# Four GNN layers over 16 batches: one layer's rows emitted beside the next batch's one-hot builds, with one scratch pool

## The chip, the cores and the metric

The kernel runs on one core of a Trainium2 chip. The metric is device time in microseconds (us), from the first to the last instruction of one execution; less is better. The engines are PE (TensorE, matmuls; PEld is its weight load), DVE (VectorE), ACT (ScalarE), POOL (GpSimd) and SP, which issues most transfers.

## The reference, cut to what matters

There are 16 batches of 1024 nodes with 128 features and a dense-stored, sparse 1024 x 1024 adjacency. Four layers run one after the other, each with a normalization ahead of it and a residual around it. Batches do not depend on each other, which is all that the change uses.

```python
x   : (16, 1024, 128) float32
adj : (16, 1024, 1024) float32, about 1.6% set, symmetric pattern, diagonal set

for layer in (L0, L1, L2, L3):
    h = maximum(layernorm(x), 0)
    x = x + layer(h, adj)

# L0: relu(concat(h, adj^T h / degree) W0^T + b0)
# L1: leaky_relu((adj / degree) h W1^T + b1)
# L2: twice: a score per edge (sigmoid of a small MLP of both ends), messages, update, layernorm
# L3: Wh = h W;  e = leaky_relu((Wh a1 + (Wh a2)^T) * (adj + I))
#     attention = softmax over the row of where(adj + I > 0, e, -1e12);  elu(attention Wh)
```

## The kernel before

The kernel treats edges, not all node pairs, in layer 2. For this it makes one-hot matrices from the adjacency, block by block, while it transposes the adjacency; I call row block `s` of this "build s". Eight builds give the transposed adjacency, the one-hots of 36 block pairs, and layer 0's neighbour sums (`acc`). Layer 2 is then two passes over eight groups of block pairs. Layer 3 walks over eight row blocks; I call each "row t".

Buffers come from pools by tag. All [128, 8, 128] float32 working tiles share tag `h` (6 buffers before), and all large PSUM tiles share tag `ps` with two buffers.

```python
def scratch(self, name):
    return self.work.tile([P, T, P], F32, tag="h", name=name, bufs=self.n_scratch)   # 6

def ps(self, name):                                                 # bufs=2
    return self.psum.tile([P, T, P], F32, tag="ps", name=name)

def layer0_own(self, xt, name):
    _, hT = self.pre_ln(xt, f"0_{name}")        # center, power on GpSimd, norm, 8 transposes, copy
    z = self.scratch(f"z0_{name}")
    nc.scalar.activation(z, self.by_node(hT, wT[:, 1], f"z0_{name}"), AF.Copy)
    own = self.scratch(f"own_{name}")
    nc.vector.tensor_add(own, self.by_node(hT, wT[:, 0], f"own_{name}"), over_t(b0_bc))
    return z, own

def layer3(self, xt, row, name):
    ...                                          # norm, wh, wh1, wh2: "the head"
    for t in range(T):                           # one row of layer 3
        at = row(t)                              # adjacency row, loaded again
        own = at[:, t * P : (t + 1) * P]
        nc.vector.tensor_add(own, own, ident)
        e = flat(self.scratch(f"e_{name}_{t}"))
        nc.vector.scalar_tensor_tensor(e, wh2, wh1[:, t : t + 1], at, op0=OP.add, op1=OP.mult)
        nc.vector.tensor_scalar(at, at, 0.0, L3_NEG, op0=OP.is_le, op1=OP.mult)
        nc.vector.scalar_tensor_tensor(e, e, L3_ALPHA, e, op0=OP.mult, op1=OP.max)
        nc.vector.tensor_add(e, e, at)
        nc.vector.tensor_reduce(nmax, e, axis=AX.X, op=OP.max, negate=True)
        nc.scalar.activation(e, e, AF.Exp, bias=nmax, accum_out=rsum[:, 0, t : t + 1])
        ps = self.ps(f"attT_ps_{name}_{t}")
        for k in range(T):
            nc.tensor.transpose(ps[:, k], e[:, k * P : (k + 1) * P], ident)
        attT = self.scratch(f"attT_{name}_{t}")
        nc.scalar.activation(attT, ps, AF.Copy)
        hp = self.one(f"hp_{name}_{t}")[:, :D]
        for k in range(T):
            nc.tensor.matmul(hp, attT[:, k], wh[:, k], start=(k == 0), stop=(k == T - 1))
        nc.vector.reciprocal(rsum[:, 1, t : t + 1], rsum[:, 0, t : t + 1])
        nc.vector.tensor_scalar(o[:, t], hp, rsum[:, 1, t : t + 1], None, op0=OP.mult)
    ...                                          # elu and residual: "the tail"

def batch(self, b):
    xt = ...                                     # load x[b]
    z, own = self.layer0_own(xt, f"{b}")
    for s in range(T):
        at = self.load_row(b, s, "at")
        nc.vector.tensor_reduce(deg[:, s : s + 1], at, axis=AX.X, op=OP.add)
        ps = self.ps(f"aT_{b}_{s}")
        for k in range(T):
            nc.tensor.transpose(ps[:, k], at[:, k * P : (k + 1) * P], ident)
        nc.scalar.activation(adjT[:, :, s * P : (s + 1) * P], ps, AF.Copy)
        for t in range(T):
            nc.tensor.matmul(acc[:, t * P : (t + 1) * P], at[:, t * P : (t + 1) * P], z[:, s], ...)
        self.build(s, at, adjT, f"{b}_{s}")      # begins with has = at OR adjT on VectorE
    self.layer0_end(xt, acc..., own, rdeg, f"{b}")
    self.layer1(xt, adjT, rdeg, f"{b}")          # begins with its own pre_ln
    self.layer2(xt, self.edge, f"{b}")           # edge: for grp in self.groups(): ...
    self.layer3(xt, lambda t: self.load_row(b, t, "a3"), f"{b}")
    ...                                          # store
```

## Time and profile before

| | before |
|---|---|
| median of 3 runs | 8855.1 us (8854.83 to 8858.05) |
| mean granted TensorE clock | 0.820 |
| one batch, end of layer 2 to end of layer 2 | 549.4 us |
| of it, layer 2 up to its last update | 267.2 us |
| of it, everything else | 282.2 us |
| loads of activation tables | 16 for Exp, 16 for Sigmoid |

Four kinds of views are used beside the page of a profile. The waits name, for an engine and a line, what ended its idle time; the numbers are us in total, how often, and the longest. The busy time by stretch gives the first and last moment of a stretch, its length, then busy us and count of instructions for PE, PEld, DVE, ACT and POOL, then the granted clock (1.00 is full), the share of DMA time and GB/s. The timeline lists start, length, engine and line of each piece of work, with the idle time before it in brackets and what ended that. The chain of work follows the work that ended last back from releaser to releaser, and lists start, length, engine, tile and line of each piece.

The busy time by stretch of the first two builds in the middle of the run, from the first VectorE operation of one build (`has`) to that of the next:

```profile
5004.40:5010.70 6.30, 6.30 (x65) 6.07 (x64) 3.47 (x10) 2.86 (x5) 0.00 (x0) 1.00 0.22 83
5010.70:5017.70 7.00, 6.36 (x65) 5.66 (x64) 4.64 (x13) 3.46 (x7) 0.00 (x0) 1.00 0.22 78
```

Build 0 and build 1 take 6.3 and 7.0 us. The later builds, with more blocks each, take 7.8, 10.7, 14.4, 15.9, 15.4 and 17.5 us.

### The profile page before, as it was taken

The page shows a single profiled execution, that of the slowest core. Times are in us where ns is not written, and L with a number is a line of the kernel's source. Part 1 is how long each engine was busy: PE and PEld are TensorE (multiplying, and loading weights), DVE is VectorE, ACT ScalarE, POOL GpSimd, SP SyncE. Part 2 cuts the span into 40 slices and gives each one's busy share as a digit, 9 for nine tenths or more (in the row PEclk, how much of TensorE's full clock was granted, in tenths as well). Part 3 has the DMA queues.
Part 4 walks back from the last instruction along what each step waited for, and adds up shares of the span by engine and source line. Part 5 has one row for each costly group of instructions (what it writes and reads, how often), then busy time and mean ns, then how long its engine had stood idle before and what let it go on. Part 6 is the DMA issues. An engine that isn't in the chain of part 4 may idle for free.

```text
span 8857.3 us, 112984 instructions
## 1 busy us (share of the span) xinstructions
PE 6284.3 (71%) x48784; PEld 4682.8 (53%) x48784; DVE 4389.8 (50%) x7991; ACT 2760.4 (31%) x4099; POOL 158.9 (2%) x105
## 2 busy tenths in 40 slices
PE   6857668576685767857678586776867768677686
PEld 5645456454554555545455454555545555455454
DVE  4454454545545455454554545445455454544544
ACT  3233242232423224232242322423224232242322
POOL 0000000000000000000000000000000000000000
PEclk8968779687896878969789697896978969789697
DMA  1010000100001000010000100001000010000100
GB/s 40 1 38 6 15 29 1 39 5 16 28 1 41 3 17 27 1 43 1 20 25 1 43 1 20 25 1 43 1 20 25 1 43 1 22 22 1 41 1 15
DMA packets 75915, 160.16 MB, mean 18 GB/s; under 512 B 6929, under 2 KB 42641, under 8 KB 75409
## 3 DMA queue, kind: packets, MB, share of 16 engines
q1 hardware_dynamic: 70144, 151.01, 5.4%
q8 instruction: 385, 6.31, 0.3%
q10 hardware_dynamic: 5264, 1.84, 0.1%
q14 instruction: 122, 0.99, 0.0%
HBM read 144.45 MB, written 8.39 MB: 17 GB/s over the span
## 4 chain that ended last, share of the span: by engine, by line
PE 64%; DVE 19%; ACT 13%; issue 2%; POOL 1%; DMA 1%; ACTq 0%; DVEq 0%; POOLq 0%; SPq 0%
PE pre L616 8%; PE sc L635 7%; PE pre L620 7%; PE p L686 7%; PE hp L323 5%; PE msg L713 5%; PE attT_ps L318 3%; PE h L262 3%; PE ga L211 3%; PE acc L746 2%; ACT hid L625 2%; ACT e L315 2%; DVE nmax L314 2%; DVE e L312 2%; ACT attT L320 1%
## 5 line engine op out<-in xcount | busy, mean ns | idle before, releaser
L625 ACT ACTIVATE hid<-pre,be_sb 128x640 f32<-128x640 f32 (+1 forms) x1152 | 880.8, 765 | 1958.2 <-PE pre L620 1939.7
L647 DVE TENSOR_SCALAR s_off<-sc,be_s 128x320 f32<-128x320 f32 x224 | 123.4, 551 | 1325.1 <-PE sc L635 1325.1
L318 PE MATMUL attT_ps<-ident,e 128*128 128x128 f32 x1024 | 252.1, 428 | 596.0 <-ACT e L315 596.0
L668 DVE TENSOR_TENSOR val<-onT,u 128x384 f32<-128x384 fp8e4 (+1 forms) x1152 | 653.4, 583 | 8.8
L635 PE MATMUL sc<-hid,slide_s 128*32 128x320 f32 (+1 forms) x4096 | 627.1, 461 | 30.3 <-ACT hid L625 30.2
L686 PE MATMUL p<-val,omT 128*128 128x128 f16 x7424 | 622.1, 218 | 10.3 <-DVE val L668 10.3
L323 PE MATMUL hp<-wh,attT 128*128 128x128 f32 x2048 | 477.1, 427 | 150.5 <-ACT attT L320 150.5
L620 PE MATMUL pre<-om,part_b 128*128 128x320 fp8e4 (+1 forms) x2304 | 540.4, 314 | 47.4 <-DVE part_b L548 28.2
L616 PE MATMUL pre<-on,part_a 128*128 128x320 fp8e4 (+1 forms) x2304 | 538.9, 315 | 32.0 <-DVE part_a L548 2.0
L686 PEld LDWEIGHTS <-omT 128*128 128x128 fp8e4 x7424 | 506.7, 96 | 85.0 <-issue 16.6
L323 PEld LDWEIGHTS hp<-wh,attT 128*128 128x128 f32 x2048 | 442.4, 328 | 201.7 <-ACT attT L320 201.7
L318 PEld LDWEIGHTS attT_ps<-ident,e 128*128 128x128 f32 x1024 | 200.9, 224 | 643.5 <-ACT e L315 643.5
L713 PE MATMUL msg<-upd,xf 128*128 128x128 f32 (+3 forms) x2944 | 539.5, 322 | 1.8 <-DVE upd L709 1.1
L668 DVE TENSOR_TENSOR val<-omT,u 128x384 f32<-128x384 fp8e4 x896 | 495.7, 553 | 0.0
L177 PE MATMUL tp<-ident,h 128*128 128x128 f32 x384 | 88.4, 408 | 549.2 <-DVE h L184 549.2
L713 PEld LDWEIGHTS msg<-upd,xf 128*128 128x128 f32 x2944 | 407.0, 191 | 121.0 <-DVE upd L709 65.3
L686 PE MATMUL p<-val,onT 128*128 128x128 f16 x5376 | 450.9, 218 | 0.0
L616 PE MATMUL pre<-on,part_b 128*128 128x320 fp8e4 x1792 | 423.4, 299 | 0.0
L531 DVE TENSOR_TENSOR omT<-pq,odd 128x384 fp8e4<-128x384 f32 (+1 forms) x576 | 329.4, 584 | 183.0 <-PE pq L528 174.5
L178 ACT ACTIVATE hT<-tp 128x1024 f32<-128x1024 f32 x64 | 65.5, 1023 | 1133.0 <-PE tp L177 1133.0
L315 ACT ACTIVATE e<-e,nmax 128x1024 f32<-128x1024 f32 x128 | 146.8, 1147 | 816.2 <-DVE nmax L314 816.2
L620 PE MATMUL pre<-om,part_a 128*128 128x320 fp8e4 x1792 | 394.8, 299 | 0.0
(202 smaller groups left out, 11164.3 us busy)
## 6 DMA issues: line engine op xcount, KB each, us to landing
at<-in_adj_dram SPq DMA_DIRECT2D x128, 512.0 KB, 3.5
a<-in_adj_dram SPq DMA_DIRECT2D x128, 512.0 KB, 3.5
x<-in_x_dram SPq DMA_DIRECT2D x16, 512.0 KB, 4.0
out_dram<-x SPq DMA_DIRECT2D x16, 512.0 KB, 3.2
wu_sb<-in_L_gnn_Wu_dram ACTq DMA_DIRECT2D x2, 256.0 KB, 5.9
we_sb<-in_L_gnn_We_dram ACTq DMA_DIRECT2D x2, 128.0 KB, 5.5
wu_sb<-in_L_gnn_Wu_dram ACTq DMA_DIRECT2D x2, 128.0 KB, 5.4
w_sb<-in_L_gnn_W_dram ACTq DMA_DIRECT2D x2, 64.0 KB, 3.2
```

The costliest lines, as they stand in the source:

```text
L211: nc.tensor.matmul(ps[:, t], mat[:, k, t * P : (t + 1) * P], z[:, k], start=(k == 0), stop=(k == T - 1),)
L315: nc.scalar.activation(e, e, AF.Exp, bias=nmax, accum_out=rsum[:, 0, t : t + 1])
L318: nc.tensor.transpose(ps[:, k], e[:, k * P : (k + 1) * P], ident)
L323: nc.tensor.matmul(hp, attT[:, k], wh[:, k], start=(k == 0), stop=(k == T - 1))
L531: nc.vector.tensor_tensor(omT, pq[:, :ck], self.odd[:, :ck, None].to_broadcast([P, ck, P]), op=OP.is_equal, saturate=False,)
L616: nc.tensor.matmul(pre[:, d, :c], ra[0][:, k, ra[1]], on[:, :c], start=(k == 0), stop=False)
L620: nc.tensor.matmul(pre[:, d, :c], rb[0][:, k, rb[1]], om, start=False, stop=(k == 1))
L625: nc.scalar.activation(hid, pre[:, :nd, :c], AF.Relu, bias=be1_sb[:, self.l : self.l + 1])
L635: nc.tensor.matmul(self.sc[g * G : (g + 1) * G, : self.c], self.path.slide[:, self.l, G - 1 - r : 2 * G - 1 - r], self.hid[self.done + g], ...
L668: nc.vector.tensor_tensor(val[:, :ck], right, u[:, :, i % J, i // J : i // J + 1].to_broadcast([P, ck, P]), op=OP.mult,)
L686: nc.tensor.matmul(self.ps[:, d * len(self.grp) + i], left[:, k], halves[:, k, :, h], start=(k == 0 and h == 0), stop=(k == self.ck - 1 an ...
L713: nc.tensor.matmul(self.msg[:, lo * P : hi * P], self.xf[:, mb], upd, start=False, stop=True, skip_group_check=True,)
```

## The change

The intent is to run the two chains of short dependent steps, layer 3's rows of batch b and the builds of batch b + 1, beside each other: after each build, one row is emitted. So that build 0 can begin at once, the start of batch b + 1 (its load, norm and layer 0's own part) moves into layer 2 of batch b, before group 3 of the second pass. Layer 3's tail moves behind layer 1. Because the lifetimes of buffers now cross, the scratch tiles, the split features of layer 2, the edge values and the adjacency rows of layer 3 all draw on one pool of 11.

```diff
-    z, own = self.layer0_own(xt, f"{b}")        # in batch(b)
+def start(self, b):
+    xt = ...                                    # load x[b]
+    return xt, *self.layer0_own(xt, f"{b}")
+
+def att_row(self, b, t, att):
+    at = flat(self.scratch(f"a3_{b}_{t}"))      # was: load_row, from the builds' three buffers
+    nc.sync.dma_start(at, adj[b, t * P : (t + 1) * P, :])
+    self.layer3_row(att, t, at, f"{b}")

# edge(), the group loop of layer 2
-    for grp in self.groups():
+    for k, grp in enumerate(self.groups()):
+        if k == 3 and l == L - 1:
+            self.during()                       # start(b + 1)

# run(), for every batch
+    att = self.layer3_head(last, f"{b - 1}") if b else None
     for s in range(T):
         ...                                     # transposes, acc
         self.build(s, at, adjT, f"{b}_{s}")
+        if b:
+            self.att_row(b - 1, s, att)
     self.layer0_end(...)
     self.layer1(xt, adjT, rdeg, f"{b}")
+    if b:
+        self.end(b - 1, last, att)              # layer 3's tail, store
     self.layer2(xt, self.edge, f"{b}")
-    self.layer3(xt, lambda t: self.load_row(b, t, "a3"), f"{b}")

# buffers
-    super().__init__(stack, 6, None)
+    super().__init__(stack, 11)                 # parts, values, wh, o and rows now come from these
-    hT = self.work.tile([P, T, P], F32, tag="hT", name=f"hT_{name}", bufs=1)
+    hT = self.work.tile([P, T, P], F32, tag="hT", name=f"hT_{name}")     # two
... (cut: layer3 split into head, row and tail; values taken in pairs)
```

## The prediction

> **What bounds the kernel now.** I read the page first (engine shares, slices), then the waits, then the busy time by stretch for one batch in the middle, then the chain of work in order of time across that batch.
>
> The page's engine shares and two of its slice rows (tenths busy, granted TensorE clock in tenths):
>
> ```profile
> PE 6284.3 (71%) x48784; PEld 4682.8 (53%) x48784; DVE 4389.8 (50%) x7991; ACT 2760.4 (31%) x4099; POOL 158.9 (2%) x105
> ...
> PE   6857668576685767857678586776867768677686
> ...
> PEclk8968779687896878969789697896978969789697
> ```
>
> No engine is full; the pattern repeats 16 times, once per batch, and the clock dips each time. One period is 549.4 us (end of layer 2 in one batch to the same point in the next). Its stages, cut where the chain changes layer: last feature update of layer 2, head of layer 3, the eight rows of layer 3, layer 0 of the next batch, the one-hot builds, the rest of layer 1, then layer 2 to the last update:
>
> ```profile
> core 0: us, PE busy (x) PEld busy (x) DVE busy (x) ACT busy (x) POOL busy (x), PEclk, DMA share, GB/s
> 4841.00:4867.50 26.50, 11.10 (x57) 7.29 (x55) 12.58 (x12) 2.23 (x2) 1.64 (x1) 0.80 0.00 0
> 4867.50:4892.70 25.20, 10.83 (x48) 7.84 (x48) 10.16 (x13) 3.10 (x4) 1.64 (x1) 0.67 0.00 1
> 4892.70:4984.10 91.40, 45.50 (x192) 40.15 (x192) 52.33 (x65) 19.37 (x25) 0.00 (x0) 0.57 0.15 46
> 4984.10:5002.50 18.40, 7.43 (x42) 7.06 (x43) 7.83 (x9) 3.10 (x3) 1.64 (x1) 0.63 0.20 58
> 5002.50:5099.40 96.90, 70.16 (x642) 57.09 (x640) 64.34 (x154) 62.90 (x125) 1.64 (x1) 0.79 0.13 44
> 5099.40:5123.20 23.80, 16.61 (x144) 16.23 (x144) 4.87 (x4) 2.03 (x3) 0.00 (x0) 1.00 0.00 1
> 5123.20:5390.40 267.20, 229.27 (x1936) 155.57 (x1936) 122.17 (x245) 79.78 (x97) 3.27 (x2) 0.94 0.00 1
> ```
>
> The reader is to see two regimes. The last row (layer 2) is TensorE-bound: 229 of 267 us busy at clock 0.94. In the other 282.2 us nothing is bound by an engine; these are chains of latencies, and rows and builds (91.4 + 96.9 us) are two such chains run one after the other. One row of layer 3 in the chain of work:
>
> ```profile
> 4906.98 1.14 DVE e L312
> 4908.15 1.23 DVE nmax L314
> 4909.40 1.25 ACT e L315 x2
> 4910.69 1.99 PE attT_ps L318 x8
> 4912.76 1.03 ACT attT L320
> 4913.84 3.79 PE hp L323 x16
> 4918.01 1.14 DVE e L312
> ```
>
> Here 11.0 us pass per row, each engine waiting for the previous one. VectorE has the eviction of the row's product ahead of the next row's add, so it too waits for the matmuls.
>
> **What the Trainium skill says.** "Perfetto Trace Analysis", Optimization Strategy, advises interleaving regimes whose most-contended engine differs: this is the change's intent, and the table agrees that there is room (52 + 64 us of VectorE in 188 us). The same page, Tensor Engine Instruction, says ACT and DVE are strict FIFO and PE reorders only weight loads; the row above agrees (VectorE idles 2.7 us before that eviction in every row while the add behind it has its operands). "TensorE: Matmul & The Clock Gate", Part 1, says idle time halves the clock; the trace agrees: eight fp32 128x128 transposes take 1.98 us in the rows (clock 0.57) and 0.88 us in the builds. "ScalarE: Activation LUTs", Table sets, says a switch of set costs a load of about 1283 ns and that abs, relu and copy are in every set: the trace has loads of 1283 ns, 16 for Exp and 16 for Sigmoid, so one of each per batch, and none between the last Exp and the builds' Abs and Copy. Mixing rows with builds should therefore add no table loads.
>
> **The change part by part**, per batch boundary; there are 15 of them, since the last batch's layer 3 still stands alone and the first batch's builds too.
>
> *Removed: layer 0's own part in the open.* Its 18.4 us (mean, norm, transposes, two products) move into the second edge pass of layer 2, before group 3: −18.4.
>
> *Removed: rows and builds in series*: −91.4 −96.9 = −188.3. *Added: both together.* VectorE has most to do. Rows: 52.3 us less three degree sums of the next batch (3 x 1.22) plus three diagonal adds that ran elsewhere (3 x 0.29) = 49.6. Builds: 64.3 plus 3.6 for those sums, less the end of layer 0 (3 x 1.22), the pre-norm of layer 1 (7.5) and the three diagonal adds (0.9) = 55.9. Together 105.5. ScalarE has 19.4 + 62.9 = 82, and TensorE 45.5 at half clock (some 22 warm) + 70 = 92. So no engine forbids 106 us. But orders are kept: rows and builds draw on the same two PSUM buffers, and the trace suggests that buffers of one tag are given in the code's order. Layer 1's normalized input is ready at 5063, yet its transposes wait for the last build's matmuls:
>
> ```profile
> 5061.90 1.13 DVE h L184
> ...
> 5095.82 0.51 PE pq L524 x4
> 5096.33 0.43 PE pq L528 x4
> 5096.76 1.71 PE tp L177 x8
> ```
>
> So build s+1 starts after row s is transposed, and a row has 5.9 us of VectorE plus 1.3 of Exp ahead of that, which must squeeze into the gaps of build s (6 to 17 us long). I choose 80% busy for VectorE (the builds alone reach 66%, with one chain): 105.5 / 0.8 = 132. Net −56.
>
> *Moved: end of layer 0 and pre-norm of layer 1.* They ran hidden inside builds 6 and 7. They take scratch buffers, which now come after row 7's in the code's order, so I expect them in the open: 3 + 6 VectorE operations of about 1.22 and the power on GpSimd 1.8 = +13.
>
> *Added to layer 2: the start of the next batch.* If its scratch and PSUM buffers come in the code's order, group 3's first gather follows the two products of the start. Group 2's scores and eight multiplies (0.55+0.5+0.4+3.8) come first, then about 7 us of mean, square, power and norm, 1 of transposes, 1 of copy, 2 + 1.8 of products: some 18 us in which TensorE has only about 2 us of messages to do. +16. If the norm slips into VectorE's 6 us gaps in group 2, this is only +6.
>
> *Added at the end: layer 3's tail*, four operations after layer 1's, mixed with layer 2's norm: +3. The rest (11 scratch buffers for values, parts and updates, two buffers for the transposed input) I count as zero: layer 2's multiplies waited only 8.8 us in all, so buffers did not bind, and two parts + four pairs + two updates are 8 of 11.
>
> Sum per boundary: −18.4 −188.3 +132 +13 +16 +3 = −42.7 us. Times 15: −640. 8855 − 640 = 8215 us.
>
> **Rivals.**
> (a) *Nearly perfect overlap.* VectorE 92% busy (115 us) and only +6 in layer 2: −70 per boundary, 7805 us. For it: TensorE warms up, so a row's matmul part shrinks from 5.8 to some 2.8 us. Against it: strict order in each queue and two PSUM buffers for four kinds of users.
> (b) *The rows are slotted between the builds rather than beside them.* Each step of build then row takes build plus some 8 us: 88 + 64 = 152, −23 per boundary, 8510 us. For it: shared PSUM order. Against it: a row's first five operations need no PSUM and VectorE idles a third of each build.
> (c) *Scratch becomes the bound.* In the joint stretch z, own, wh, wh2 and o hold five of 11; in layer 2 the held z and own leave nine. If multiplies wait for a pair, TensorE in layer 2 starves, and 5% of layer 2's 267 us is 13 us. With (b) that gives about 8700, no gain to speak of. Against it: one row holds only three buffers.
> (d) *Transfers.* A row of layer 3 now loads into scratch: 3.5 us to landing, DMA share 0.15; I count it as hidden.
>
> **Range and chances.** The middle is 8215; I round to 8210. The range runs from near (a), 7850, to (b), 8510. Over 2% faster means below 8678, which takes only 12 us per boundary: 0.90. Within 2% needs (b) and (c) together: 0.07. Slower needs more than 12 us per boundary lost: 0.03.
>
> **What would show it.** Period near 507 us. Joint stretch some 130 us long with VectorE near 80% and the clock above 0.8; eight row transposes near 0.9 us, not 1.98. A hole of 12 to 18 us in TensorE's work within the second edge pass, before group 3. The norm of layer 1 in the open after the last row. Still 16 + 16 table loads. The prediction is wrong if builds start during layer 3's head (much faster), if the hole is absent, if VectorE stays near 66% in the joint stretch, or if layer 2's multiplies begin to wait for buffers.

## More of the kernel before

One line of the waits of the kernel before is the most useful one here:

```profile
PE attT_ps L318 <- ACT e L315: 596.0, 128, 8.1
```

TensorE waits for the exponentials before the transposes of every one of the 128 rows, 596 / 128 = 4.7 us each. This is idle time that other work could fill.

## The result and the profile after

The changed kernel takes 8494.9 us (median of 4 runs, 8492.1 to 8503.1), the kernel before 8856.1 (4 runs, 8854.8 to 8858.1). All outputs are right. All ratios here are the mean time of one kernel's runs over that of the other's of the same rounds, so not quite the ratio of the medians: 0.9594, with a 95% interval of 0.9577 to 0.961. The change is faster, by 361 us, and the time lies inside the predicted range. But the middle of the prediction was a gain of 645 us; 0.56 of it came. The time is close to rival (b), 8510.

The page of the kernel after, engine shares and two slice rows:

```profile
PE 6197.0 (73%) x48784; PEld 4623.5 (54%) x48784; DVE 4291.8 (51%) x7991; ACT 2754.0 (32%) x4099; POOL 158.9 (2%) x105
...
PE   6867768677786777867778677776777768777684
...
PEclk8988879788797888979889798897988879888796
```

The counts of instructions are those of before; what changed is order and buffers. The mean clock is 0.844 instead of 0.820; the dips are still there.

The busy time by stretch of one batch in the middle: last update of layer 2, head of layer 3, rows and builds together, norm of layer 1 in the open, rest of layer 1, then layer 2 in three pieces, of which the middle one runs from one group's scores to the next group's around the start of the next batch:

```profile
4658.90:4685.20 26.30, 14.93 (x94) 11.63 (x94) 13.80 (x13) 2.23 (x2) 1.64 (x1) 0.85 0.08 21
4685.20:4707.80 22.60, 11.68 (x51) 8.77 (x52) 7.85 (x10) 2.09 (x3) 1.64 (x1) 0.65 0.00 0
4707.80:4855.40 147.60, 100.54 (x777) 84.15 (x775) 102.85 (x211) 82.77 (x150) 0.00 (x0) 0.76 0.16 54
4855.40:4863.80 8.40, 0.10 (x1) 0.00 (x0) 6.41 (x8) 0.00 (x0) 1.64 (x1) 0.67 0.00 0
4863.80:4895.70 31.90, 21.94 (x152) 21.05 (x152) 7.59 (x8) 3.10 (x3) 0.00 (x0) 0.77 0.01 2
4895.70:5094.20 198.50, 162.36 (x1310) 109.03 (x1310) 85.80 (x161) 58.16 (x71) 3.27 (x2) 0.91 0.02 6
5094.20:5126.00 31.80, 19.90 (x150) 15.37 (x151) 12.07 (x19) 6.11 (x8) 1.64 (x1) 0.79 0.00 1
5126.00:5184.60 58.60, 56.17 (x517) 39.55 (x516) 31.08 (x74) 17.48 (x22) 0.00 (x0) 1.00 0.01 1
```

In the third row VectorE is busy for 102.85 of 147.6 us, 70% and not the 80% that I had chosen. Set against the table in the prediction, stage by stage (in the kernel before I put the end of the builds at 5096.7, where layer 1's transposes begin, since that is the point where the fifth row here begins; the prediction had cut 2.7 us later):

| stage, us per batch | before | after | difference | predicted |
|---|---|---|---|---|
| last update | 26.5 | 26.3 | −0.2 | 0 |
| head of layer 3 | 25.2 | 22.6 | −2.6 | 0 |
| rows, layer 0's own part, builds | 204.0 | 147.6 | −56.4 | −74.7 |
| end of layer 0 and norm of layer 1 in the open | 0 | 8.4 | +8.4 | +13 |
| layer 1 from its transposes, with the tail | 26.5 | 31.9 | +5.4 | +3 |
| layer 2 to its last update | 267.2 | 288.9 | +21.7 | +16 |
| sum | 549.4 | 525.7 | −23.7 | −42.7 |

Fifteen times −23.7 is −356 us, which is the whole result of −361 within its spread. Of the 19 us per batch that are missing, 18.3 lie in the third line: 15.6 because the joint stretch is that much longer than the 132 us predicted, and 2.7 because of the prediction's later cut, which counted the first transposes of layer 1 as saved. The other lines miss by less than 6 us each, and partly cancel.

Where the joint stretch loses time shows when it is cut at each build's `has`. The first three steps in the kernel after:

```profile
4709.70:4728.20 18.50, 11.04 (x64) 9.83 (x64) 9.22 (x18) 6.62 (x9) 0.00 (x0) 0.72 0.16 58
4728.20:4748.70 20.50, 11.64 (x75) 10.26 (x75) 11.86 (x24) 6.76 (x11) 0.00 (x0) 0.75 0.14 51
4748.70:4762.30 13.60, 9.32 (x78) 7.93 (x78) 9.09 (x21) 7.90 (x14) 0.00 (x0) 0.87 0.24 78
```

The steps with a row in them take 18.5, 20.5, 13.6, 16.3, 16.9, 17.7, 20.1 and 20.7 us, against builds alone of 6.3, 7.0, 7.8, 10.7, 14.4, 15.9, 15.4 and 17.5. (The last step is cut at 4854.0, where the end of layer 0 is done; the eviction of row 7's product ends 1.5 us later.) Steps 0 and 1 pay 12.2 and 13.5 us for their row, more than the 11.0 us that a row took on its own. Steps 2 to 7 pay 3.9 on average. No engine is busy for more than 60% of step 0 or 1.

The chain of work in order of time through step 0 tells why (pieces of issue time and short ones left out):

```profile
4714.31 3.52 PE acc L780 x16
4717.83 0.44 PE pm L549 x4
...
4718.30 0.57 ACT om L552
4718.89 1.28 ACT L323
4720.18 1.25 ACT e L323 x2
...
4721.47 1.81 PE attT_ps L326 x8
```

L323 without a name is the load of the Exp table, and `e` at 4720.18 is row 0's Exp. Its row maximum is ready at 4718.9, just as build 0's last copy (`om`) ends; the table's load then stands ahead of it, and it is done at 4721.4. TensorE's timeline, from its last matmul of build 0 (`pm`) on:

```profile
4721.47 1.80 PE L326 MATMUL attT_ps<-ident,e 128*128 128x128 f32 x8 [3.21 <-ACT e L323]
4723.07 1.27 PE L777 MATMUL aT<-ident,at 128*128 128x128 f32 x5
4724.39 2.38 PE L331 MATMUL hp<-wh,attT 128*128 128x128 f32 x16
4726.61 0.49 PE L777 MATMUL aT<-ident,at 128*128 128x128 f32 x3
```

After `pm` TensorE is idle for 3.2 us until row 0's transposes can run. Build 1's transposes (`aT`) need only the loaded adjacency, yet five of the eight come after the row's transposes and three after its product. Build 1's `has` follows at 4728.19. So step 0 is a build, then an Exp, then a row: one after the other, as rival (b) had it.

In step 1 TensorE waits 4.3 us for row 1's Exp in the same way, and in steps 2 to 7 it waits for no Exp. The 38 such waits of the whole run are these two at each of the 15 boundaries and the eight rows of the last batch.

Steps 1 to 4 hold another wait. The neighbour sums (`acc`) of the row three builds further on stand between a build's own products in TensorE's order, and that row has not landed yet: 0.8, 2.5, 2.1 and 2.0 us at this boundary, 7.4 together. In the whole run, before and after:

```profile
PE acc L746 <- DMA at<-in_adj_dram: 1.8, 2, 1.1
PE acc L780 <- DMA at<-in_adj_dram: 113.8, 61, 3.1
```

These loads lie on the chain of work in steps 1 to 4. No experiment below removes this wait alone, so what it costs is not shown.

The second loss, in layer 2, is as expected in kind. The timeline of the kernel after, DVE and PE pieces around the start of the next batch (others left out):

```profile
5099.59 0.55 DVE L684 TENSOR_TENSOR val<-omT,u 128x384 f32<-128x384 fp8e4 x1
5100.05 1.22 DVE L166 TENSOR_TENSOR cen<-x,st 128x1024 f32<-128x1024 f32 x1
...
5107.17 1.94 PE L177 MATMUL tp<-ident,h 128*128 128x128 f32 x8 [9.76 <-DVE h L184]
...
5115.80 0.43 PE L629 MATMUL pre<-on,part_a 128*128 128x320 fp8e4 x2
```

TensorE, the bound of layer 2, waits 9.8 us for the norm, and the next group's gather (`pre`) comes after both products. From scores to scores this takes 31.8 us where a neighbouring interval takes 11.9: a hole of 19.9 us, for work that had taken 18.4 us in the open.

### The profile page after: what moved, and what is told of

It reads as the page before. It is cut to its first block, busy times and chain, and to the rows that moved or that the text cites. A ratio compares the mean times of both kernels' runs of the same rounds, so it can differ in the third digit from the quotient of the medians.

```text
span 8491.8 us, 112613 instructions
## 1 busy us (share of the span) xinstructions
PE 6197.0 (73%) x48784; PEld 4623.5 (54%) x48784; DVE 4291.8 (51%) x7991; ACT 2754.0 (32%) x4099; POOL 158.9 (2%) x105
## 4 chain that ended last, share of the span: by engine, by line
PE 59%; DVE 21%; ACT 11%; issue 4%; DMA 3%; POOL 2%; ACTq 0%; POOLq 0%; DVEq 0%; SPq 0%
PE pre L629 8%; PE sc L648 7%; PE pre L633 7%; PE p L702 6%; PE msg L729 5%; PE ga L211 3%; PE acc L780 3%; PE hp L331 3%; PE h L262 3%; DMA at<-in_adj_dram 3%; ACT hid L638 2%; PE attT_ps L326 2%; ACT e L323 1%; PE tp L177 1%; ACT attT L328 1%
## 5 line engine op out<-in xcount | busy, mean ns | idle before, releaser
L780 PE MATMUL acc<-z,at 128*128 128x128 f32 x2048 | 377.8, 350 | 113.8 <-DMA at<-in_adj_dram 113.8
L535 PE MATMUL pq<-rank,on 128*128 128x128 f16 x1856 | 273.4, 281 | 241.8 <-DVE on L530 169.2
L178 ACT ACTIVATE hT<-tp 128x1024 f32<-128x1024 f32 x64 | 65.5, 1023 | 1159.2 <-PE tp L177 1159.2
L780 PEld LDWEIGHTS acc<-z,at 128*128 128x128 f32 x2048 | 343.3, 256 | 126.8 <-DMA at<-in_adj_dram 124.4
L177 PEld LDWEIGHTS tp<-ident,h 128*128 128x128 f32 x384 | 75.3, 223 | 592.3 <-issue 464.6
L546 ACT ACTIVATE onT<-pq 128x384 fp8e4<-128x384 f32 (+1 forms) x576 | 298.2, 518 | 283.8 <-DVE omT L542 283.8
L629 PEld LDWEIGHTS <-part_a 128*128 128x128 f16 x2304 | 184.4, 97 | 371.1 <-issue 333.5
```

Source lines behind the costliest of these rows:

```text
L535: nc.tensor.matmul(pq[:, i], on[:, i * P : (i + 1) * P], rank[:, t], start=True, stop=True)
L546: nc.scalar.activation(onT, pq[:, 4 : 4 + ck], AF.Copy, saturate=False)
L629: nc.tensor.matmul(pre[:, d, :c], ra[0][:, k, ra[1]], on[:, :c], start=(k == 0), stop=False)
```

## The experiments

The comparison of the traces leaves three things to explain: the hole in layer 2, the norm in the open, and the length of the joint stretch. For the last one, two theories stood against each other: VectorE has too little time (then fewer VectorE operations help by their full length), or the order in which rows and builds stand in the queues costs (then moving code helps, with the same operations).

### The start of the next batch after layer 2 again

```diff
-            if k == 3 and l == L - 1:
-                self.during()
...
             self.layer2(xt, self.edge, f"{b}")
+            if b + 1 < B:
+                begun = self.start(b + 1)
```

> Undoes one part: the next batch's norm and two products come after layer 2 again, as before, with everything else of the change kept. Theory (the move bought nothing, since the hole of 19.9 us in the second edge pass is as long as the 18.4 us it replaced): 8495 us within 1.5%, that is 8370 to 8620, and the group interval of 31.8 us in the second pass back at 11.9. Rival (the move is worth its 18 us per boundary and the hole has another cause): about 8495 + 15 x 18 = 8765, and the hole stays.

Measured: 8387.4 us, ratio to before 0.9468 (0.9453 to 0.9484). Undoing this part of the change gains 108 us over the kernel after, 7.2 us per boundary. The hole is gone, and the start, now in the open, costs less than the 18.4 us it took before the change: from the update's `msgT` to the end of layer 2 32.0 us instead of 26.3, and from there to the first build 30.6 instead of 24.5, so 11.8 us together, because its norm runs between the operations of the last update. What follows: moving the start into layer 2, as it was done, was itself a loss.

### The start of the next batch in four pieces

```diff
+    # start_parts(b): center | norm, transposes | z | own, with a yield after each
             g.dots(i)
+            if l == L - 1 and i == 2 and 2 <= k <= 5:
+                next(self.during, None)
```

> Same work at the same place, but in four pieces (mean and square; norm and transposes; first product; second product), each in the middle of another group of the second edge pass, so that each is ready when its turn for the two PSUM buffers comes. Theory (the hole is TensorE waiting in order for the whole chain of the start): the four groups take about 12 + 1.5 us each instead of one with 31.8, so 14 to 16 us less per boundary, 8255 to 8285 us. Rival (the start costs layer 2 its engine time and buffers, wherever it stands): within 60 us of 8495.

Measured: 8338.8 us, 0.9409 (0.9394 to 0.9425): 156 us less than the kernel after, 10.4 us per boundary and not 14 to 16. The four intervals between scores are 14.7, 15.7, 15.5 and 12.1 us, where the kernel after has 31.8 and three times 11.9. Their sum is 9.4 us less. So the pieces still cost 10.5 us in a stage that TensorE bounds, some of it the TensorE work itself.

### Without the row maximum

On these inputs the result still agrees with the reference.

```diff
-            nc.vector.tensor_reduce(nmax, e, axis=AX.X, op=OP.max, negate=True)
-            nc.scalar.activation(e, e, AF.Exp, bias=nmax, accum_out=rsum[:, 0, t : t + 1])
+            nc.scalar.activation(e, e, AF.Exp, accum_out=rsum[:, 0, t : t + 1])
```

> The row maximum (one VectorE operation of 1.21 us per row) is left out; Exp runs without it, results stay the same to rounding since the scores are small. Theory (in the joint stretch VectorE's row operations lie on the path, because they are put in order between the small operations that a build's chain needs): 8 x 1.2 = 9.7 us less per boundary and some 10 us for the last batch, so about 8340 us. Rival (VectorE is idle 30% of the stretch, so an operation less is hidden; PSUM order or loads set the pace): less than 40 us gained.

Measured: 8366.6 us, 0.9441 (0.9425 to 0.9456): 128 us less than the kernel after, 8.5 us per boundary of the 9.7 us of VectorE work that were removed there. (The last batch's rows, which stand alone, take part in this.) Taken alone this looks like a VectorE bound. But the operation is also a link of each row's chain, ahead of its Exp, so this run does not tell the theories apart.

### One more VectorE operation per row, beside the chain

```diff
             nc.vector.tensor_reduce(nmax, e, axis=AX.X, op=OP.max, negate=True)
+            nc.vector.tensor_reduce(spare, at, axis=AX.X, op=OP.max, negate=True)
```

Its result is not used; it costs VectorE 1.2 us per row.

> One more VectorE operation per row, a maximum over the adjacency row of about 1.21 us into a buffer that nothing reads, so that it lengthens no row's chain. Theory (VectorE's time in the stretch is on the path): + 9.7 us per boundary, about 8640 to 8650 us. Rival (it fills idle time of VectorE): within 50 us of 8495.

Measured: 8557.2 us, 0.9655 (0.9639 to 0.9672): 62 us more than the kernel after, 4.1 us of the 9.7 per boundary. That lies between the two expectations. The operation was not wholly beside the chain, though. In the code it stands after the row maximum, but the compiled order has it ahead of the maximum in four of the eight rows of the boundary that I looked at (0, 1, 2 and 7). In row 0:

```profile
4747.97 1.21 DVE L324 TENSOR_REDUCE spare<-a 128x1 f32<-128x1024 f32 x1
4749.10 1.21 DVE L322 TENSOR_REDUCE nmax<-e 128x1 f32<-128x1024 f32 x1
```

In rows 0 and 1 it took the place of the degree sum, which moved behind the maximum, and steps 0 and 1 take 18.5 and 20.5 us as in the kernel after: in the two steps that lose most, it cost nothing. Step 6 grew from 20.1 to 22.3. (Without the row maximum, steps 0 and 1 took 16.1 and 19.6 us.) Over half of its time fell into gaps. VectorE's length alone does not set the joint stretch.

### A row's product one build later

The row is split into its softmax (to the Exp) and its product (transposes and matmul), and the product of row s − 1 comes after build s.

```diff
     self.build(s, at, adjT, f"{b}_{s}")
     if b:
-        self.att_row(b - 1, s, att)
+        if s:
+            self.layer3_product(att, s - 1, e, f"{b - 1}")
+        e = self.att_row(b - 1, s, att)          # now only the softmax
```

> Only the order in the code changes: a row's transposes and product come one build later than its softmax, so build s, product of row s-1, softmax of row s. Theory (steps 0 and 1 of the joint stretch cost 12 to 13 us more than their builds alone, because the next build's transposes stand behind a row whose Exp is not ready, in a short build; from step 2 on a row costs 2 to 6 us): steps 0 and 1 shrink to builds plus some 6 us each, row 7's product is exposed at the end by some 5 us, net 7 to 10 us less per boundary, 8345 to 8390 us. Rival (the rows cost VectorE time, which the order of products does not change): within 40 us of 8495.

Measured: 8539.7 us, 0.9641 (0.9625 to 0.9657): 45 us slower than the kernel after, where I expected 105 to 150 us less. The steps are 7.4, 11.0, 21.3, 15.4, 17.6, 18.4, 19.2 and 33.1 us. The first two did shrink, from 18.5 and 20.5, as the theory has it. But row 1's softmax began only at 4758.2, 7.3 us after build 2's `has`, and not beside build 1; and the last row, with its product behind it, made the last step 12 us longer. The gain at the front was given back.

### End of layer 0 and norm of layer 1 before the last build

```diff
+    if s == T - 1:                               # the last acc is complete here
+        nc.vector.reciprocal(rdeg, deg)
+        self.layer0_end(...)
+        h1 = self.layer1_norm(xt, f"{b}")        # center and norm, without the transposes
     self.build(s, at, adjT, f"{b}_{s}")
```

> Only the order in the code changes: the end of layer 0 and the norm of layer 1 come before build 7 instead of after row 7. Theory (scratch buffers are handed out in the code's order, so in the changed kernel these operations could not slip under the last builds as they did before): the 8.4 us norm in the open disappears, and the end of layer 0 with it, 8 to 11 us less per boundary, 8330 to 8375 us. Rival (they wait for VectorE, which is full there): within 40 us of 8495.

Measured: 8448.4 us, 0.9538 (0.9522 to 0.9554): 47 us less than the kernel after, 3.1 us per boundary of the 8.4 that stood in the open, and not the 8 to 11 that I expected. The norm did leave the open, but its VectorE operations now stand ahead of row 7's, whose first long operation starts 16.8 us after the last `has` instead of 2.1.

### Rows and builds in series again, with everything else of the change

```diff
     att = self.layer3_head(last, f"{b - 1}") if b else None
+    if b:
+        for t in range(T):
+            self.att_row(b - 1, t, att)
...
         self.build(s, at, adjT, f"{b}_{s}")
-        if b:
-            self.att_row(b - 1, s, att)
```

> The mixing alone is undone: all eight rows come before the builds in the code, the rest of the change stays. Theory (the mixing turned 91.4 + 96.9 us in series into 147.6): about 41 us more per boundary less some overlap at the seam, 8950 to 9110 us, so slower than the kernel before. Rival (the gain comes from the larger scratch pool and the moved start, and the mixing brings little): below 8700 us.

Measured: 9321.6 us, 1.0525 (1.0508 to 1.0543), slower than expected and slower than before by 5%. The kernel after is 827 us faster, 55 us per boundary, and the rest of the change alone is a loss. But the 827 us are not all overlap: a row in series takes 14.6 us here and 11.0 before. Eight rows make 29 of the 55 us, and if all 128 rows of the run are like this one, they make 461 us, nearly all of the 465 us by which this run is slower than the kernel before. VectorE's timeline in this run (a row's eviction, the next row's first long operation, the next eviction):

```profile
4613.62 0.35 DVE L333 TENSOR_SCALAR o<-hp,rsum 128x128 f32<-128x128 f32 x1 [6.82 <-PE hp L331]
4614.20 1.28 DVE L315 SCALAR_TENSOR_TENSOR e<-wh,wh,a 128x1024 f32<-128x1024 f32 x1
...
4628.21 0.35 DVE L333 TENSOR_SCALAR o<-hp,rsum 128x128 f32<-128x128 f32 x1 [6.82 <-PE hp L331]
```

Each row's first operations come after the previous row's eviction, and VectorE is idle for 6.8 us ahead of that. In the kernel before, four of the next row's operations ran in this gap. The only differences for a row are where its buffers come from (the shared pool instead of the three row buffers that it had in common with the builds, and `wh` and `o` in the pool), so I put the new order down to the shared pool. I did not isolate it.

### The three repairs together

The edits are those of the four pieces, of the late product and of the early end of layer 0, in one kernel:

```diff
+            if l == L - 1 and i == 2 and 2 <= k <= 5:
+                next(self.during, None)
...
+        if s == T - 1: ...                       # layer0_end, layer1_norm
         self.build(s, at, adjT, f"{b}_{s}")
+        if s: self.layer3_product(att, s - 1, e, f"{b - 1}")
+        e = self.att_row(b - 1, s, att)
```

> The three repairs together: products one build later, end of layer 0 and norm of layer 1 before build 7, start of the next batch in four pieces. If the three losses are separate (hole, first two steps, norm in the open) the gains add: 10 + 8 + 9 = some 27 us per boundary, about 8090 us. If VectorE becomes the bound of the joint stretch, part of it is lost: 8200 us or more.

Measured: 8375.3 us, 0.9457 (0.9441 to 0.9473), far from 8090. With the late product in it, it is slower than the four pieces alone.

### The late product, with the rows' loads on another queue

The loads of the builds and of the rows share the queue of SP, and in the kernel after a build's load waits there for its buffer (34 us at most). My theory for the late row 1 was that its load stood behind such a wait.

```diff
-        nc.sync.dma_start(at, adj[b, t * P : (t + 1) * P, :])
+        nc.gpsimd.dma_start(at, adj[b, t * P : (t + 1) * P, :])
```

> The products one build later, as in e5, and the rows' adjacency loads issued from the GpSimd queue instead of the SyncE queue. Theory (e5 gained nothing because row 1's and row 7's loads stood in the SyncE queue behind loads of the builds' rows that waited for a free row buffer; row 1 landed some 15 us late, at 4757 instead of 4741, and the rows shifted by one build to the end): step 2 of the joint stretch shrinks from 21.3 to about 14 us and the last from 33 to about 26, some 12 us less per boundary than e5, 8330 to 8390 us. Rival (the joint stretch is a sum of VectorE's and the chains' times that the order only moves about): within 50 us of e5's 8540.

Measured: 8551.7 us, 0.966 (0.9644 to 0.9676), and row 1 starts as late as before. The theory fell: row 1 does not start late because of the queue of the loads. TensorE's waits for the builds' rows ahead of `acc` did halve, from 68.7 to 32.1 us in all, without a gain.

### Four pieces and early end of layer 0, without the late product

```diff
+            if l == L - 1 and i == 2 and 2 <= k <= 5:
+                next(self.during, None)
...
+        if s == T - 1: ...                       # layer0_end, layer1_norm
         self.build(s, at, adjT, f"{b}_{s}")
         if b:
             self.att_row(b - 1, s, att)          # softmax and product, as in the kernel after
```

> The two repairs that helped alone, together: start of the next batch in four pieces (e2: -156 us) and end of layer 0 and norm of layer 1 before build 7 (e6: -47 us). They lie in different stretches, so they should add: about 8290 us.

Measured: 8299.6 us, 0.9368 (0.9353 to 0.9384), as expected: these two repairs add up.

### All of it, with the rows' loads on another queue

```diff
         self.build(s, at, adjT, f"{b}_{s}")
+        if s: self.layer3_product(att, s - 1, e, f"{b - 1}")
+        e = self.att_row(b - 1, s, att)
...
-        nc.sync.dma_start(at, adj[b, t * P : (t + 1) * P, :])
+        nc.gpsimd.dma_start(at, adj[b, t * P : (t + 1) * P, :])
```

> e9 with both repairs of e10. If e9's theory holds and the gains add, about 8150 to 8200 us; if e9 gains nothing, about 8330 us, the level of e8.

Measured: 8344.0 us, 0.9419 (0.9404 to 0.9435), the rival's figure. The late product in this form, with the other queue, costs 44 us against the run without them on the same chip. Against the three repairs on one queue (0.9457, on another chip) it gains 0.0038, some 34 us; there the waits ahead of `acc` went from 70.7 to 31.9 us in all. So the loads may cost something, but these two pairs of runs do not agree on it.

### The next row's softmax ahead of the late product

The late product had row s's softmax after the product of row s − 1 in the code. Both take scratch buffers: the softmax its row and `e`, the product `attT`. If a buffer is given in the code's order, the softmax's comes free only after the product has taken its own. This version has build s, then softmax s, then product s − 1; the two other repairs are in it as well.

```diff
     self.build(s, at, adjT, f"{b}_{s}")
     if b:
-        self.att_row(b - 1, s, att)
+        ahead = self.att_row(b - 1, s, att)      # softmax of row s
+        if s:
+            self.layer3_product(att, s - 1, e, f"{b - 1}")
+        e = ahead
```

> e10 with the products one build later, but each row's softmax now stands before the previous row's product in the code. In e5 and e9 it stood after it, and row 1's softmax came one build late (at 4758, with the loads of another queue too), as scratch buffers handed out in the code's order would do: row 1's adjacency buffer after row 0's transposed copy. In the compiled order row 1's first operation now stands inside build 1. Theory (the first two steps lose 12 us each because build s+1's transposes wait behind a row whose Exp is not ready): steps 0 and 1 take some 9 and 13 us instead of 18.5 and 20.5, step 2 grows by 3, row 7's product adds 3 at the end, net 9 to 12 us less per boundary than e10, 8120 to 8165 us. Rival (the stretch is a sum of rows' and builds' times that order only moves about): 8260 us or more.

Measured: 8046.2 us (8038.6 to 8055.2), 0.9087 (0.9072 to 0.9102). The run with the same two other repairs had 0.9368; the difference of 0.0281 times 8855 is 249 us, from order alone. It was taken on another chip, so I compare the ratios. The three repairs together (0.9457) differ from this version in nothing but the order of softmax s and product s − 1 in the code: that order is worth 0.0370, 328 us. It is the best version, and the gain is larger than expected.

The waits of TensorE for the Exp of a row, first in the kernel after, then in the run with four pieces and early end of layer 0, then in this one:

```profile
PE attT_ps L326 <- ACT e L323: 169.0, 38, 9.4
```

```profile
PE attT_ps L335 <- ACT e L332: 224.8, 53, 9.4
```

```profile
PE attT_ps L339 <- ACT e L332: 65.5, 12, 9.4
```

Six of the twelve waits that are left, and 46.0 of the 65.5 us, fall in the last 96 us of the run, where the last batch's rows stand alone. At the boundary shown next TensorE waits for no Exp at all; at one of the run with two repairs it waits for three, 10.7 us. The busy time by stretch of this run, its first three steps and then from the first `has` to 5090.0, just before the matmuls of row 6's product:

```profile
4956.20:4963.60 7.40, 4.35 (x27) 4.12 (x28) 6.46 (x14) 1.99 (x4) 0.00 (x0) 0.58 0.38 143
4963.60:4979.50 15.90, 11.26 (x90) 9.96 (x89) 12.12 (x25) 9.87 (x16) 0.00 (x0) 0.87 0.18 68
4979.50:4995.20 15.70, 10.74 (x86) 9.80 (x86) 13.17 (x26) 8.11 (x14) 0.00 (x0) 0.78 0.21 68
...
4956.20:5090.00 133.80, 89.50 (x730) 75.24 (x730) 106.55 (x213) 78.37 (x145) 1.67 (x1) 0.77 0.17 60
```

The same first three steps in the run with the two other repairs alone:

```profile
4597.40:4615.80 18.40, 10.92 (x64) 9.80 (x64) 9.22 (x18) 6.64 (x10) 0.00 (x0) 0.72 0.16 58
4615.80:4636.20 20.40, 12.72 (x75) 11.20 (x75) 11.87 (x24) 6.88 (x11) 0.00 (x0) 0.67 0.15 51
4636.20:4650.60 14.40, 10.40 (x77) 9.26 (x78) 9.17 (x21) 7.99 (x14) 0.00 (x0) 0.76 0.21 74
```

They take 39.0 us together against 53.2. Row 0's Exp, which still loads its table first, ends at 4967.8, inside build 1, and TensorE is at build 1's work by then. Row 0's transposes follow at 4973.3, wait for nothing, and take 1.04 us. From the first `has` to the start of layer 1's transposes it is 138.6 us, against 151.5 in the run with two repairs and 154.2 in the kernel after. In the stretch shown VectorE is busy for 106.55 of 133.8 us, 80%. The whole 138.6 us have 108.53, 78%, and the 151.5 us of the run with two repairs have 108.61, 72%: the share came from the order, with the same operations.

## Why the prediction was right or wrong

**What bounds the kernel: right.** The rows and builds were chains of latencies, and mixing them paid: from the first build to the end of the rows 147.6 us instead of 91.4 + 94.2 in series. (The 827 us against the same kernel without the mixing include rows that are slower there.) No engine became the bound.

**Rows and builds together: the step that failed.** "I choose 80% busy for VectorE ... 105.5 / 0.8 = 132." VectorE's work was sized well (102.85 us measured, 3.7 of them the end of layer 0, which the prediction had outside), but it was busy for 70%, and the stretch took 147.6 us: 15.6 us more per boundary. With the 2.7 us of the later cut the term misses by 18.3 us, 275 us in all, nearly the whole miss of 285. In its place the runs showed an order: row s stands ahead of build s + 1 for TensorE, and when its Exp is not ready, build s + 1 waits. In steps 0 and 1 the builds are too short to hide a row's chain with the Exp and its table load, and those steps pay 12.2 and 13.5 us. The extra operation shows that VectorE's length is only in part the cause (4.1 of 9.7 us, and nothing in steps 0 and 1), and the softmax ahead of the late product, with the same operations, gives 249 us back, 14.2 of its 16.6 us per boundary in the first three steps. I had named the mechanism ("build s+1 starts after row s is transposed") and then put it into one share of busy time, where it should have been worked out per step: short builds cannot hide a row.

**Rival (b): near in time, in part by luck.** It set the slow end of the range, and the measured time lies 15 us inside that. But two steps pay more than its 8 us for a row (12.2 and 13.5) and six pay less (3.9), which came out near its sum.

**The start of the next batch in layer 2: right in kind.** +16 predicted; the hole is 19.9 us and layer 2 grew by 21.7. What I did not see is that the −18.4 us for taking it out of the open was the wrong comparison: left after layer 2, it would have cost 11.8 us beside the update.

**End of layer 0 and norm of layer 1 in the open: right in kind,** 8.4 us where I had 13; the end of layer 0 ran beside row 7's product. **Tail of layer 3:** 5.4 us where I had 3, in a layer 1 whose clock is now 0.77. **Head:** 2.6 us less, which I had not counted.

**Table loads and layer 2's scratch: right in count; transfers: not settled.** There are 16 + 16 loads, as before. (Their 1283 ns, which the prediction puts under Table sets, stand in the section "What ACT_TABLE_LOAD costs" of the same page.) The multiplies of layer 2 waited 8.8 us in all before and after, so rival (c) did not come. But the load of the Exp table, which I counted as nothing new, lies on the chain in step 0, and TensorE now waits 113.8 us in all for the adjacency ahead of `acc`, some 7.5 us per boundary. That is a form of rival (d), which I had counted as hidden. It lies on the chain, and stays in the best version (85.7 us); what it costs was not tested by itself, so part of the 15.6 us may be its.

**Clock in the joint stretch: wrong.** I expected above 0.8 and row transposes of 0.9 us per eight; it was 0.76. The eight of rows 0 and 1, which follow a wait, took 1.80 and 1.97 us, those of rows 2 to 4 1.05 to 1.09. (The 0.88 us that the prediction gives for the builds is counted by the chain from the end of the matmul before; the timeline has 1.04.) What kept the clock low is not shown: the best version, without these waits, has 0.77 in its stretch.

**What stays open.** That the shared pool gives buffers in the code's order, and that this made rows alone slower and row 1 late in the late product, agrees with all runs but was not isolated: neither 13 scratch buffers nor a fourth buffer for adjacency rows fitted beside the one-hots (such kernels do not build). The best version gained another 3.8 us per boundary outside the joint stretch; 2.8 of them lie between the start of layer 1's transposes and its first VectorE operation (20.8 us against 23.6, at a clock of 1.00 against 0.93), the rest was not followed up.

## What to carry to other kernels

When two chains of latencies are emitted alternately, work out each step of the alternation by itself: what stands next in an engine's order, and whether its operand will be ready by then. Emit the consumer of a late operand one step later, and the next step's producer ahead of it in the code: the late product alone lost 45 us, and with the producer first it gained. Before moving work into a stage that an engine bounds, ask what it costs where it is, once its neighbours there can overlap with it.

## What the Trainium skill lacked or had wrong

- "Perfetto Trace Analysis", Optimization Strategy, advises interleaving regimes, and the runs agree (8494.9 us with it, 8856.1 before). It lacks that the order within each queue then decides the gain: the same operations took 0.9368 of the time before in one order and 0.9087 in another.
- No page says what it costs when a change of pools goes with another order on an engine: with rows and builds in series, a row took 14.6 us instead of 11.0, with VectorE idle for 6.8 us ahead of each eviction (that the pool is the cause was not isolated).
- "TensorE: Matmul & The Clock Gate", Part 4, says of transposes that the fast clock "doesn't engage" for them, and gives about 275 ns for one of bf16. Here eight fp32 transposes took 1.97 us in the timeline of the kernel before's rows (clock 0.57 over the rows) and 1.04 us in its builds 1 and 2 (clock 1.00), so beside other matmuls their time does follow the clock. Whether transposes alone would raise the clock no run shows.
- No page says that work moved into a stage that TensorE bounds can cost more than in the open: 19.9 us in layer 2 in one piece, 10.5 in four pieces, 11.8 in the open after it.
